# A two-layer graph attention kernel: 36 row gathers move into the prologue, and each of 36 steps computes one chunk of table rows itself

## The chip, the cores and the metric

The kernel runs on one core of one Trainium2 chip. The metric is the device time of one execution in microseconds (us). The core has a matrix engine (PE, with its weight loads PEld), a vector engine (DVE), a scalar engine (ACT), a general engine (POOL, GpSimd) that here mostly issues indirect DMAs, and SP, which issues plain DMAs. Each engine works through its own instructions in order and waits on semaphores of the others; 16 DMA engines carry all transfers.

## The reference, cut to what matters

The graph has N = 6250 nodes with 256 features and E = 200,000 edges sorted by destination, plus a self loop at every node. What is computed, in float32:

```
h  = relu(layernorm(x))                       # per node
for l, heads in ((0, 4), (1, 1)):
    hx  = x_l @ Wg                            # x_0 = h; 256 x 256, per node
    te  = relu(edge_attr @ We + be) * exp(x_l @ Wo + bo)[src]
    al  = leaky_relu((hx.as)[src] + (hx.ad)[dst] + (te @ Wge).ae, 0.2)
    al  = softmax of al over the edges of each dst
    out = segment_sum(hx[src] * al, dst) + b
    x_l+1 = relu(out + x_l) if l == 0 else out + x_l
return x + x_2 + h
```

## The kernel before

**Tables.** Every edge needs the row of its source node: hx (256 numbers), the logit parts and exp(x Wo + bo). The prologue (`prologue`) makes these rows once for all nodes and stores them in a DRAM table `T[0]`, 268 numbers a row; layer 0 makes the table `T[1]` for layer 1 as its nodes get done.

**Steps.** The edges are cut into 66 superchunks per layer: 64 of 24 chunks of 128 edges, and two short ones at the end (14 and 13 chunks), 1563 chunks in all. One superchunk of one layer is a step. `edges` writes the order of the work of all 132 steps out by hand; there is no scheduler. While step k (`st`) is computed, step k+1 (`nx`) is fetched and prepared, and the nodes of step k-1 (`pv`) are finished; `late` is the step whose T[1] rows are still to be multiplied and stored.

**The gather.** `gather(nx)` issues one indirect DMA on POOL per chunk: 128 table rows into `G[:, c, :]`. There are three G buffers, used in turn, so the gathers of step k+3 need the matmuls of step k to be done.

**Inside a step**, in order: `logits` (DVE, needs all chunks of G), `ends` (a PE transpose), `spread` and `parts` (one-hot masks and destination terms for `nx`), `rphase1` (edge features of `nx`: PE, ACT), `links` (two short scans on DVE and a PE transpose), `rows2(late)` (two PE matmuls for T[1]), `blocks`, `maxima` (DVE, ending with an Exp on ACT), `rphase2` and `adst` (PE), `scale` (layer 0: one 6.5 us DVE multiply; layer 1: 24 ACT copies), `carried`, `sums` (24 matmuls on PE), `rows3(late)` (bias add on DVE, stores on SP), `onehots(nx)`, `finish(pv)`, `evict`, `rows1(pv)` (PE transposes, ACT copy into `h1T`), `edge_rows(nx)`.

**The prologue.** 49 tiles of 128 nodes in 9 groups (2, 5, then 7 each, 5, 2 tiles). Per tile: layernorm statistics on DVE (`stats`), normalise on ACT (`norm`), two PE transposes and an ACT copy (`turn`), two PE matmuls (`mult`), bias add on DVE (`keep`). The reciprocal root of the variance is a bit trick and three Newton steps, on DVE for groups 0 to 2 and on POOL for groups 3 to 8. Per group, SP loads x (`load`) and stores the rows (`store`); three row buffers `trow` alternate. Then come 24 more tiles: the x rows that the 24 chunks of superchunk 0 need are gathered straight from x on POOL during the prologue (`first_rows`, `NX = 24`) into the first G buffer, and go through the same tile work in place. So step 0 needs no table; steps 1 to 131 do.

Of the kernel before, what the change touches and what calls it, by code (L numbers as in the profile page):

```python
# [31 lines left out]
P = 128  # L32
C = 24
SE = P * C
NX = 24
D = 256
ED = 32
PH = 64
# [41 lines left out]
class Kernel:  # L80
# [10 lines left out]
    def run(self):  # L91
        nc, tc = self.nc, self.tc
        self.cp = self.pool("consts")
        self.dp = self.pool("tables", space=DRAM)
        N = self.N
        self.T = [self.dp.tile([N + P, L.TW], F32, name=f"T{L.l}") for L in self.L]
        n, w = (self.NS + 1) // 2, self.L[1].TW + D
        self.nd = [self.dp.tile([n * (M + 1), w], F32, name=f"nd{i}") for i in range(2)]
        self.x1 = self.dp.tile([N + P, D], F32, name="x1")
        with ExitStack() as c:  # L100
            c.enter_context(tc.manual_schedule())
            self.gp = [self.pool("gath0", 1, c)]
# [3 lines left out]
            self.steps = [dict(L=L, s=s, C=self.cs[s], o=offs[s], k=L.l * self.NS + s)  # L106
                          for L in self.L for s in range(self.NS)]
            self.prologue()
            self.edges(c)
        self.general()  # L110


    def consts(self, wp):
# [5 lines left out]
        pool = (wp, cp)  # L119
        self.ones = cp.tile([P, 1], F32, name="ones")  # L120
        nc.gpsimd.memset(self.ones, 1.0)
        self.bias, self.webd, self.be, wge = [], [], [], []
        def weights(L):

# [79 lines left out]
    def prologue(self):  # L204
# [7 lines left out]
        with ExitStack() as c:  # L212
# [15 lines left out]
            src0 = wp.tile([P, CX], I32, name="src0", bufs=1)  # L228
            nc.sync.dma_start(src0, a["src"][:, 0:CX])
            for g in range(1, 3):  # L230
                load(g)
            first, later, more = self.consts(wp)
# [18 lines left out]
            self.G0 = G0 = self.gp[0].tile([P, C, 270], F32, name="G")  # L251

            def first_rows():
                for i in range(CX):
                    nc.gpsimd.indirect_dma_start(
                        out=G0[:, i, 0:D], out_offset=None, in_=a["x"][0:N, :],
                        in_offset=bass.IndirectOffsetOnAxis(ap=src0[:, i:i + 1], axis=0))
                    yield

            rows0 = first_rows()  # L260
# [5 lines left out]
            def stats(g):  # L266

                n, x = len(groups[g]), xs[g]
                w = GT if g < g0 else C
                st = wp.tile([P, w, 6], F32, name=f"st{w}", bufs=2 if g < g0 else 1)  # L270
                mv = wp.tile([P, w, 2], F32, name=f"mv{w}", bufs=3 if g < g0 else 1)
                s = wp.tile([P, 3, w], F32, name=f"sc{w}", bufs=3 if g < g0 else 1)
                for i in range(n):
                    V.bn_stats(st[:, i, :], x[:, i, :])
                    yield
                for i in range(n):
                    V.bn_aggr(mv[:, i, :], st[:, i, :])
# [6 lines left out]
                V.tensor_scalar(y.bitcast(I32), v.bitcast(I32), -0.5, float(0x5F3759DF), op0=OP.mult, op1=OP.add)  # L284
                yield
                V.tensor_scalar(v, v, -0.5, None, op0=OP.mult)
                yield
                e = nc.gpsimd if 3 <= g < g0 else V
                for _ in range(3):
                    e.tensor_mul(t, y, y)  # L290
# [5 lines left out]
                    if e is V:  # L296
                        V.scalar_tensor_tensor(y, t, 1.5, y, op0=OP.add, op1=OP.mult)
                        yield
                    else:
                        e.tensor_scalar(t, t, 1.5, None, op0=OP.add)  # L300
                        e.tensor_mul(y, t, y)
                e.tensor_copy(out[:, :, 0], y)
                if e is V:
                    V.scalar_tensor_tensor(out[:, :, 1], mv[:, :n, 0], -1.0, y, op0=OP.mult, op1=OP.mult)
                else:
                    e.tensor_mul(t, mv[:, :n, 0], y)
                    e.tensor_scalar(out[:, :, 1], t, -1.0, None, op0=OP.mult)
                yield

# [51 lines left out]
                        del ahead[q]  # L361

            index = self.indices(wp)
            kept = 0
# [279 lines left out]
    def edges(self, ctx):  # L644
# [30 lines left out]
        for k, st in enumerate(steps):  # L675
# [199 lines left out]
    def gather(self, st):  # L875
# [4 lines left out]
        for c in (range(0) if st["k"] == 0 and self.CX > last else (last, *range(last))):  # L880
            nc.gpsimd.indirect_dma_start(  # L881
                out=G[:, c, 0:L.TW], out_offset=None, in_=self.T[L.l][0:self.N, :],
                in_offset=bass.IndirectOffsetOnAxis(ap=idx[:, c:c + 1], axis=0))

    def pair(self, k):

# [411 lines left out]
        e.tensor_add(nrow, nrow, b)  # L1298
        yield

    def turned(self, st, wp, psum):
        pT = psum.tile([P, 512], F32, name="fin")
        for i in range(2):
            self.nc.tensor.transpose(pT[:, i * P:(i + 1) * P], st["x1"][:, i * P:(i + 1) * P], self.ident)
        st["hT"] = hT = wp.tile([P, 2, P], F32, name="h1T", bufs=1)
        self.nc.scalar.activation(hT.rearrange("p k n -> p (k n)"), pT[:, :2 * P], AF.Copy)  # L1306

# [168 lines left out]
def drain(g):  # L1476
    for _ in g:
        pass
# [22 lines left out]
def layout(inputs):  # L1501
# [23 lines left out]
    for s, c in enumerate(cs):  # L1525
        e0, e1 = o * P, (o + c) * P
        nx[e1 - 1] = END_DST
        for t, v in ((srcp, sp), (dstp, dp), (dnxp, nx)):
# [11 lines left out]
        o += c  # L1540
    a.update(gsrc=sp.reshape(-1, 1), gdst=gdst.reshape(-1, 1), gdrow=gdst,
             gea=np.ascontiguousarray(eap.T))
    a.update(src=srcp, dst=dstp, dnx=dnxp, drow=drow, prow=prow, sdst=sdst,
             dpv=np.ascontiguousarray(prow[:, 3].T),
             srow=np.ascontiguousarray(sp[:cs[0] * P].reshape(P, -1).T),
# [26 lines left out]
```

## Time and profile before

| | |
|---|---|
| median of 3 runs | 4050.89 us (4050.79 to 4054.03) |
| profiled execution | 4055.1 us, its span 4053.3 us |
| POOL busy | 2998.9 us (74%) |
| PE busy | 2639.2 us (65%) |
| DVE busy | 2436.3 us (60%) |
| ACT busy | 1117.1 us (28%) |
| granted PE clock, mean | 0.779 |

Busy time leaves out register, branch, semaphore and DMA-issuing instructions of SP; an indirect DMA on POOL does count. Times in the views count from the span's start. Layer 0 runs from about 115 to 2067 us and layer 1 from there to the end. A row of grouped instructions gives line, engine, operation, output and input, count, then busy us and mean ns of one, then the engine's idle time before them and what ended it. A timeline row gives start, length, engine, line, operation, output and input, count and, in brackets, the idle time before it with its releaser.

### The profile page before, as it was taken

What the parts mean: (1) busy time and instruction counts of PE and PEld (TensorE: products, weight loads), DVE (VectorE), ACT (ScalarE), POOL (GpSimd) and SP (SyncE); (2) the same over time, 40 slices, a digit from 0 to 9 for tenths busy, and PEclk for the clock granted to TensorE, in tenths of its full rate; (3) what the DMA queues carried; (4) which work ended last, traced back from release to release, by engine and by line L of the source; (5) the groups of instructions that cost most, each with busy time, mean ns of one, the idle gap of its engine ahead of it and who ended that gap; (6) DMA issues with size and microseconds to landing.
All of it is one profiled execution on the core that took longest, in us unless ns stands there. A gap on an engine that the chain in (4) does not pass through costs nothing.

```text
span 4053.3 us, 37237 instructions
## 1 busy us (share of the span) xinstructions
PE 2639.2 (65%) x9878; PEld 1719.8 (42%) x9878; DVE 2436.3 (60%) x6063; ACT 1117.1 (28%) x2670; POOL 2998.9 (74%) x3253
## 2 busy tenths in 40 slices
PE   8776766666666766766646656656656566566565
PEld 6454444444444444444433433434434334334343
DVE  7887877877877877877744434333344343343445
ACT  5211111111111111111123434434334344343341
POOL 5777777777777777777747777777777777777775
PEclk9888878888887888888777777777777777777777
DMA  7455555555555555555534455455445445445443
GB/s 246 135 158 143 150 155 144 150 154 146 149 154 149 147 152 151 146 151 153 138 108 134 136 143 142 131 142 141 134 139 141 135 138 144 132 138 143 134 136 96
DMA packets 239250, 583.15 MB, mean 144 GB/s; under 512 B 64235, under 2 KB 96401, under 8 KB 238971
## 3 DMA queue, kind: packets, MB, share of 16 engines
q0 software_dynamic: 150144, 422.75, 39.3%
q1 hardware_dynamic: 88477, 157.30, 12.1%
q8 instruction: 85, 1.39, 0.1%
q14 instruction: 128, 1.05, 0.1%
q10 hardware_dynamic: 416, 0.67, 0.1%
HBM read 542.72 MB, written 37.86 MB: 143 GB/s over the span
## 4 chain that ended last, share of the span: by engine, by line
POOL 33%; DVE 27%; issue 14%; ACT 9%; PE 9%; DMA 8%; DVEq 0%; SPq 0%; ACTq 0%; POOLq 0%
POOL G L881 33%; DVE G L1192 8%; DMA G<-T,src 7%; ACT G L1201 7%; PE y L981 4%; DVE S L1021 4%; PE u L1211 2%; DVE lb L1005 2%; PE ps L439 1%; DVE m L1140 1%; DVE rt L1070 1%; ACT R L982 1%; DVE al L1088 1%; DVE al L1086 1%; DVE fb L1101 1%
## 5 line engine op out<-in xcount | busy, mean ns | idle before, releaser
L881 POOL DMA_INDIRECT G<-T,src x3102 | 2946.7, 950 | 1003.3 <-issue 916.3
L1211 PE MATMUL u<-G,S 128*128 128x270 f32 (+1 forms) x6252 | 1569.1, 414 | 187.4 <-DVE G L1182 184.1
L1211 PEld LDWEIGHTS u<-G,S 128*128 128x128 f32 x6252 | 1279.1, 206 | 479.0 <-DVE G L1182 212.2
L1201 ACT ACTIVATE G<-G,kw 128x256 f32<-128x256 f32 x1512 | 609.0, 497 | 0.0
L982 ACT ACTIVATE R<-y,webd 128x1024 f32<-128x1024 f32 (+2 forms) x264 | 235.4, 892 | 1322.8 <-PE y L981 817.4
L1108 PE MATMUL lf<-ident,fb 128*36 128x128 f32 (+1 forms) x132 | 50.3, 381 | 821.3 <-DVE fb L1101 795.7
L1084 DVE TENSOR_TENSOR G<-rt,G 128x96 f32<-128x96 f32 (+1 forms) x132 | 30.3, 230 | 866.0 <-DMA G<-T,src 866.0
L1192 DVE TENSOR_TENSOR G<-G,kps 128x6144 f32<-128x6144 f32 (+3 forms) x77 | 440.9, 5734 | 0.0
L1021 DVE TENSOR_TENSOR S<-kps,loc 128x3072 f32<-128x3072 f32 x132 | 437.6, 3315 | 4.6
L981 PE MATMUL y<-ea,webd 64*128 64x256 f32 (+1 forms) x1056 | 393.7, 840 | 50.9 <-ACT R L982 50.9
L990 PE MATMUL zad<-R,wea 128*64 128x384 f32 (+1 forms) x1056 | 308.2, 726 | 158.5 <-ACT R L982 158.2
L1108 PEld LDWEIGHTS lf<-ident,fb 128*36 128x36 f32 (+1 forms) x132 | 15.8, 119 | 863.4 <-DVE fb L1101 837.0
L990 PEld LDWEIGHTS zad<-R,wea 128*64 128x64 f32 x1056 | 88.2, 189 | 428.3 <-ACT R L982 339.8
L1216 ACT ACTIVATE U<-u 128x270 f32<-128x270 f32 (+1 forms) x132 | 51.8, 393 | 631.0 <-PE u L1211 631.0
L1243 DVE SCALAR_TENSOR_TENSOR mg<-U,mw 128x1 f32<-128x1 f32 x66 | 14.5, 220 | 281.3 <-ACT mw L1241 281.3
L981 PEld LDWEIGHTS y<-ea,webd 64*128 64x128 f32 x1056 | 124.7, 289 | 123.7 <-ACT R L982 70.3
L1174 DVE SCALAR_TENSOR_TENSOR G<-U,kw,G 1x257 f32<-1x257 f32 x62 | 29.6, 478 | 185.1 <-ACT G L1201 185.1
L1070 DVE STREAM_TRANSPOSE rt<-zad 128x768 f32<-128x768 f32 (+1 forms) x130 | 126.1, 970 | 8.5 <-PE zad L1056 8.5
L1042 PE MATMUL zad<-a,Q 128*128 128x12 bf16 (+1 forms) x132 | 26.1, 197 | 156.6 <-DVE a L1037 156.2
L439 PE MATMUL fin<-wg,h1T 128*128 128x260 f32 x264 | 125.3, 623 | 3.7 <-ACT h1T L1306 3.7
L1005 DVE TENSOR_TENSOR lb<-lb,kps 128x1536 bf16<-128x1536 bf16 (+1 forms) x68 | 112.9, 1661 | 0.0
L1316 ACT ACTIVATE t1row<-t1row 128x1 f32<-128x1 f32 x66 | 13.4, 203 | 349.9 <-DVE t1row L443 349.9
(195 smaller groups left out, 2238.4 us busy)
## 6 DMA issues: line engine op xcount, KB each, us to landing
G<-T,src POOLq DMA_INDIRECT x3102, 2.8
ea<-in_ea_dram SPq DMA_DIRECT2D x64, 768.0 KB
lb<-locrow SPq DMA_DIRECT2D x64, 384.0 KB
nd<-t1row SPq DMA_DIRECT2D x66, 225.8 KB
tw<-nd SPq DMA_DIRECT2D x66, 225.8 KB
tw<-T SPq DMA_DIRECT2D x66, 117.2 KB
T<-t1row SPq DMA_DIRECT2D x66, 113.8 KB
tw<-in_x_dram SPq DMA_DIRECT2D x66, 112.0 KB
```

The lines of the kernel that those rows point to most:

```text
L439: self.nc.tensor.matmul(ps[:, :L.MW], hT[:, k, :], self.wg[L.l][:, k, :], start=(k == 0), stop=(k == 1))
L881: nc.gpsimd.indirect_dma_start(out=G[:, c, 0:L.TW], out_offset=None, in_=self.T[L.l][0:self.N, :], in_offset=bass.IndirectOffsetOnAxis(ap= ...
L981: nc.tensor.matmul(y[:, i, :n], self.webd[l][r, :], ea[r, w], start=True, stop=True)
L982: nc.scalar.activation(R[:, :, w], y[:, :, :n], AF.Relu, bias=self.be[l])
L990: nc.tensor.matmul(st["zad"][i * PH:(i + 1) * PH, o], self.wea[l][0], R[:, i, w], start=True, stop=False)
L1005: V.tensor_tensor(lb[:, :, :n], lb[:, :, :n], self.k_part.unsqueeze(2).to_broadcast([P, i, n]), op=OP.is_equal)
L1021: nc.vector.tensor_tensor(st["S"][:, c0:c1, :], self.k_iota.unsqueeze(1).to_broadcast(w), self.loc[:, o + c0:o + c1].unsqueeze(2).to_broad ...
L1070: V.transpose(rv[:, :32 * c].rearrange("p (b n) -> p b n", b=2), z.rearrange("p (b n) -> p b n", b=2)[:, :, :16 * c])
L1108: self.nc.tensor.transpose(self.lf[0:e.shape[1], 1:P + 1], e, self.ident)
L1192: nc.vector.tensor_tensor(v, v, pw[:, c0:c1, :].unsqueeze(3) .to_broadcast([P, c1 - c0, H, L.F]), op=OP.mult)
L1201: self.nc.scalar.activation(v, v, AF.Copy, scale=st["w"][:, c:c + 1])
L1211: nc.tensor.matmul(st["u"][:, :L.W], S[:, i, :], G[:, i, 0:L.W], start=(j == 0), stop=(j == c - 1))
```

## The change

- `NX` falls from 24 to 12: chunks 0 to 11 of superchunk 0 still come from x in the prologue; chunks 12 to 23 are gathered from the table after it. The prologue has 61 tiles instead of 73.
- For steps 1 to 36 of layer 0 (`early`), the prologue gathers the x rows of the last chunk on POOL, 36 gathers, into slots 12 to 23 of the first G buffer, used three times over; after every four gathers SP stores them to a DRAM tensor `xg` (9 stores of 512 KB). A slot is written again only when its store has landed. `begun < 7 + 17 * k // 20` paces the 48 prologue gathers over the tiles. A new input `srcx` holds their indices.
- In those 36 steps `gather` issues 23 indirect DMAs, and SP loads the 128 x rows from `xg` into `G[:, 23, :]` (128 KB, one plain DMA). The step then does the tile work for this chunk, for `nx`: `early_norm` behind `ends` (4 DVE and 13 ACT instructions), `early_turn` behind `blocks` (two PE transposes and an ACT copy into `h1T`), `early_mult` ahead of `rphase2` (two PE matmuls), `early_keep` ahead of `sums` (a DVE add, an ACT Exp).
- `rows2(late)` moves from behind `links` to ahead of `spread`, `rows3(late)` from behind `sums` to behind `links`, in all steps of both layers. The new work uses the same single `fin` buffer of PSUM and the same `h1T` as they and `rows1` do.
- In the prologue's Newton steps POOL keeps groups 3, 5 and 7; groups 4, 6 and 8 go to DVE, and the last Newton product is written in place of a copy.

```diff
-NX = 24
+NX = 12
+NB = 36
+EB = 4
...
             def first_rows():
-                for i in range(CX):
+                for i in range(NR):
+                    j = i - CX
+                    q = i if j < 0 else CX + j % NE
                     nc.gpsimd.indirect_dma_start(
-                        out=G0[:, i, 0:D], out_offset=None, in_=a["x"][0:N, :],
+                        out=G0[:, q, 0:D], out_offset=None, in_=a["x"][0:N, :],
                         in_offset=bass.IndirectOffsetOnAxis(ap=src0[:, i:i + 1], axis=0))
+                    b = j % EB
+                    if j >= 0 and (b == EB - 1 or i == NR - 1):
+                        nc.sync.dma_start(self.xg[:, j - b:j + 1, :], G0[:, q - b:q + 1, 0:D])
                     yield
...
-                e = nc.gpsimd if 3 <= g < g0 else V
+                e = nc.gpsimd if g in (3, 5, 7) and g < g0 else V
...
-                if 0 <= k < 10 or k >= 14 and k % 4 == 0:
+                while begun < 7 + 17 * k // 20:
+                    begun += 1
                     next(rows0, None)
...
             drain(self.logits(st))
             self.ends(st)
+            self.early_norm(nx)
+            if late:
+                self.rows2(late)
             self.spread(nx)
             self.parts(nx)
             y = self.rphase1(nx)
             next(y)
             self.links(st)
             if late:
-                self.rows2(late)
+                self.rows3(late)
+                late = None
             self.load_fl(k + 1)
             self.blocks(nx)
+            self.early_turn(nx)
             drain(self.maxima(st))
             drain(y)
+            self.early_mult(nx)
             self.load_ea(k + 2)
             self.rphase2(nx)
...
             self.carried(st)
+            self.early_keep(nx)
             self.sums(st)
-            if late:
-                self.rows3(late)
-                late = None
...
+        if L.l == 0 and st["s"] in self.early:
+            nc.sync.dma_start(G[:, last, 0:D], self.xg[:, self.early[st["s"]], :])
+            st["x"] = G[:, last, :]
+            order = range(last)
...
+    def early_norm(self, st):
+
+        if "x" not in st:
+            return
+        V, L, x = self.nc.vector, st["L"], st["x"][:, 0:D]
+        act = self.nc.scalar.activation
+        t = self.wp.tile([P, 12], F32, name="xt")
+        mean, var, y, q, b = (t[:, i:i + 1] for i in range(6, 11))
+        V.bn_stats(t[:, 0:6], x)
+        V.bn_aggr(t[:, 6:8], t[:, 0:6])
+        V.tensor_scalar(var, var, EPS, None, op0=OP.add)
+        V.tensor_scalar(y.bitcast(I32), var.bitcast(I32), -0.5, float(0x5F3759DF), op0=OP.mult, op1=OP.add)
+        act(var, var, AF.Copy, scale=-0.5)
+        act(mean, mean, AF.Copy, scale=-1.0)
+        for _ in range(3):
+            act(q, y, AF.Copy, scale=y)
+            act(q, q, AF.Relu, bias=self.c15, scale=var)
+            act(y, q, AF.Copy, scale=y)
+        act(b, mean, AF.Copy, scale=y)
+        st["h"] = h = self.np_.tile([P, D], F32, name="hw", bufs=2)
+        self.nc.scalar.activation(h, x, AF.Relu, bias=b, scale=y)
...
+    def early_mult(self, st):
+
+        if "x" in st:
+            st["t0"] = self.ps_f.tile([P, 512], F32, name="fin")
+            self.node_rows(st["L"], st["hT"], st["t0"])
+
+    def early_keep(self, st):
+
+        if "x" in st:
+            L, row = st["L"], st["x"]
+            self.node_store(L, st["t0"], row)
+            self.nc.scalar.activation(row[:, L.g:L.g + 1], row[:, L.g:L.g + 1], AF.Exp)
```

More of the change, by code (lines that the diff above doesn't have):

```diff
@@ L107, in run @@
                           for L in self.L for s in range(self.NS)]
+            n = min(NB, self.NS - 4) if self.cs[0] >= NX + EB else 0
+            self.early = {s: s - 1 for s in range(1, n + 1)}
+            if self.early:
+                self.xg = self.dp.tile([P, len(self.early), D], F32, name="xg")
             self.prologue()
@@ L121, in consts @@
         nc.gpsimd.memset(self.ones, 1.0)
+        self.c15 = cp.tile([P, 1], F32, name="c15")
+        nc.gpsimd.memset(self.c15, 1.5)
         self.bias, self.webd, self.be, wge = [], [], [], []
@@ L227, in prologue @@
             load(0)
-            src0 = wp.tile([P, CX], I32, name="src0", bufs=1)
-            nc.sync.dma_start(src0, a["src"][:, 0:CX])
+            NR, NE = CX + len(self.early), (self.cs[0] - CX) // EB * EB
+            src0 = wp.tile([P, NR], I32, name="src0", bufs=1)
+            nc.sync.dma_start(src0, a["srcx"][:, 0:NR])
             for g in range(1, 3):
@@ L287, in stats @@
                 yield
-                e = nc.gpsimd if 3 <= g < g0 else V
-                for _ in range(3):
+                e = nc.gpsimd if g in (3, 5, 7) and g < g0 else V
+                for i in range(3):
+                    z = out[:, :, 0] if i == 2 else y
                     e.tensor_mul(t, y, y)
@@ L295, in stats @@
                         yield
-                    if e is V:
-                        V.scalar_tensor_tensor(y, t, 1.5, y, op0=OP.add, op1=OP.mult)
+                        V.scalar_tensor_tensor(z, t, 1.5, y, op0=OP.add, op1=OP.mult)
                         yield
@@ L300, in stats @@
                         e.tensor_scalar(t, t, 1.5, None, op0=OP.add)
-                        e.tensor_mul(y, t, y)
-                e.tensor_copy(out[:, :, 0], y)
+                        e.tensor_mul(z, t, y)
                 if e is V:
-                    V.scalar_tensor_tensor(out[:, :, 1], mv[:, :n, 0], -1.0, y, op0=OP.mult, op1=OP.mult)
+                    V.scalar_tensor_tensor(out[:, :, 1], mv[:, :n, 0], -1.0, out[:, :, 0], op0=OP.mult, op1=OP.mult)
                 else:
-                    e.tensor_mul(t, mv[:, :n, 0], y)
+                    e.tensor_mul(t, mv[:, :n, 0], out[:, :, 0])
                     e.tensor_scalar(out[:, :, 1], t, -1.0, None, op0=OP.mult)
@@ L363, in prologue @@
             index = self.indices(wp)
-            kept = 0
+            kept, begun = 0, 6
             for k in range(-3, len(tiles) + 1):
@@ L879, in gather @@
         last = st["C"] - 1
-        for c in (range(0) if st["k"] == 0 and self.CX > last else (last, *range(last))):
+        first = self.CX if st["k"] == 0 else 0
+        order = (last, *range(first, last)) if first <= last else ()
+        if L.l == 0 and st["s"] in self.early:
+            nc.sync.dma_start(G[:, last, 0:D], self.xg[:, self.early[st["s"]], :])
+            st["x"] = G[:, last, :]
+            order = range(last)
+        for c in order:
             nc.gpsimd.indirect_dma_start(
@@ L883, in gather, with early_turn @@
                 in_offset=bass.IndirectOffsetOnAxis(ap=idx[:, c:c + 1], axis=0))
+    def early_norm(self, st):
[18 more added lines that the diff above has]
+        self.nc.scalar.activation(h, x, AF.Relu, bias=b, scale=y)
+    def early_turn(self, st):
+        if "x" in st:
+            self.turned(st, self.np_, self.ps_f, st["h"])
+    def early_mult(self, st):
[3 more added lines that the diff above has]
+    def early_keep(self, st):
+        if "x" in st:
+            L, row = st["L"], st["x"]
+            self.node_store(L, st["t0"], row)
+            self.nc.scalar.activation(row[:, L.g:L.g + 1], row[:, L.g:L.g + 1], AF.Exp)
     def pair(self, k):
@@ L1299, in nodes0, with turned @@
         yield
-    def turned(self, st, wp, psum):
+    def turned(self, st, wp, psum, x=None):
+        x = st["x1"] if x is None else x
         pT = psum.tile([P, 512], F32, name="fin")
         for i in range(2):
-            self.nc.tensor.transpose(pT[:, i * P:(i + 1) * P], st["x1"][:, i * P:(i + 1) * P], self.ident)
+            self.nc.tensor.transpose(pT[:, i * P:(i + 1) * P], x[:, i * P:(i + 1) * P], self.ident)
         st["hT"] = hT = wp.tile([P, 2, P], F32, name="h1T", bufs=1)
@@ L1542, in layout @@
              gea=np.ascontiguousarray(eap.T))
+    early = [offs + c - 1 for offs, c in zip(np.cumsum([0] + cs).tolist(), cs)][1:NS - 3]
+    a.update(srcx=np.ascontiguousarray(srcp[:, [*range(min(cs[0], NX)), *early[:NB]]]))
     a.update(src=srcp, dst=dstp, dnx=dnxp, drow=drow, prow=prow, sdst=sdst,
```

## The prediction

> **What bounds the kernel now.** I read the page first (busy shares by engine, the 40 slices, the group of gathers), then who waited for whom on POOL, then POOL's instructions in order of time. The page:
>
> ```profile
> PE 2639.2 (65%) x9878; PEld 1719.8 (42%) x9878; DVE 2436.3 (60%) x6063; ACT 1117.1 (28%) x2670; POOL 2998.9 (74%) x3253
> POOL 5777777777777777777747777777777777777775
> L881 POOL DMA_INDIRECT G<-T,src x3102 | 2946.7, 950 | 1003.3 <-issue 916.3
> ```
>
> POOL looks only 74% busy, evenly. But of the 1003.3 us in which it stood idle before a gather, 916.3 are "issue": it waited for nothing. The waits of POOL say the same, and give the three real stops:
>
> ```profile
> POOL G L881 <- issue: 916.3, 3008, 0.3
> POOL G L881 <- DMA T<-t1row: 40.1, 1, 40.1
> POOL G L881 <- DMA tw<-in_x_dram: 14.3, 1, 14.3
> POOL G L881 <- ACT pen L972: 4.8, 1, 4.8
> ```
>
> 40.1 us is the change of layer, where the table must be complete. The other two lie at the start. In order of time on POOL:
>
> ```profile
> 72.73 0.95 POOL L255 DMA_INDIRECT G<-in_x_dram,src  x1 [0.30 <-issue]
> 88.01 0.94 POOL L881 DMA_INDIRECT G<-T,src  x1 [14.34 <-DMA tw<-in_x_dram]
> 89.26 0.95 POOL L881 DMA_INDIRECT G<-T,src  x1 [0.31 <-issue]
> ...
> 147.01 0.94 POOL L881 DMA_INDIRECT G<-T,src  x1 [0.30 <-issue]
> 152.73 0.95 POOL L881 DMA_INDIRECT G<-T,src  x1 [4.78 <-ACT pen L972]
> ```
>
> A gather costs 1.25 us from start to start (88.01 to 89.26). POOL starts when the stores of T[0] have landed, runs 48 gathers (steps 1 and 2) to 147.01, and stops once, at step 3, for the first G buffer, which step 0 still uses. So the end is: start of the table gathers, plus 1.25 us for each of 3102, plus the stops, plus a tail. Everybody else waits for POOL. DVE's wait in the whole run, then in layer 0 from 400 to 1200 us, then busy times there (PE, PEld, DVE, ACT, POOL):
>
> ```profile
> DVE G L1084 <- DMA G<-T,src: 866.0, 121, 19.6
> ```
> ```profile
> DVE G L1084 <- DMA G<-T,src: 131.5, 26, 9.6
> ```
> ```profile
> 800.00:1200.00 400.00, 270.74 (x989) 176.41 (x986) 310.98 (x671) 55.02 (x131) 303.11 (x319) 0.82 0.54 151
> ```
>
> In layer 0 a step lasts 24 x 1.25 = 30.0 us, so 800 us are 26.7 steps, and DVE waits 131.5 / 26.7 = 4.9 us a step for gathers. Its own work with its small waits takes 25.1 us. That is the room the change has in a step.
>
> **The change part by part.**
>
> *Gathers after the prologue.* 36 steps issue 23 instead of 24: 36 x 1.25 = -45.0 us. Step 0 gathers 12 chunks from the table that came from x before: 12 x 1.25 = +15.0 us. Net -30.0 us of POOL, if POOL stays the bound.
>
> *The stop at step 3* (4.8 us) goes. Step 0 needed its G buffer until 152; with POOL 15 us of gathers later at step 3 and step 0 having 12 tiles less to wait for, the buffer is free well before: -4.8 us. What is late next there is POOL itself.
>
> *The start of the table gathers.* The prologue gets 48 instead of 24 x gathers, nine stores to xg, and two chains between them. Rows of the prologue: two of POOL in order of time around a Newton block, the landing of x gathers, the last three stores of T on SP, the first 88 us and a full stretch (PE to POOL busy, then PE clock, DMA share, GB/s), and the two DMA queues in the first 88 us:
>
> ```profile
> 29.27 0.21 POOL L290 TENSOR_TENSOR sc<-sc 128x7 f32<-128x7 f32 x1 [3.34 <-DVE sc L284]
> 33.68 1.07 POOL L255 DMA_INDIRECT G<-in_x_dram,src  x1 [0.17 <-issue]
> ```
> ```profile
> DMA to landing us min/median/max: 2.7/5.5/8.5
> ```
> ```profile
> 74.81 8.39 SPq L344 DMA_DIRECT2D T<-trow  x3
> ```
> ```profile
> 0.00:88.00 88.00, 75.62 (x344) 55.88 (x344) 72.55 (x325) 50.43 (x129) 50.23 (x149) 0.98 0.78 257
> 30.00:40.00 10.00, 8.80 (x46) 6.84 (x45) 5.01 (x22) 6.52 (x18) 3.70 (x14) 1.00 1.04 266
> ```
> ```profile
> q1 hardware_dynamic: 6063, 18.67, 62.5%
> q0 software_dynamic: 1152, 3.15, 12.3%
> ```
>
> A Newton block takes POOL 33.68 - 29.27 = 4.4 us. The new order on POOL is 13 gathers, block 3, 12 gathers, block 5, 11 gathers, block 7, 12 gathers. From the end of block 3 at 33.7: 33.7 + 15.0 + 4.4 + 13.8 + 4.4 + 15.0 = 86.3, if nothing holds it. The last gather starts at 85.0 and lands 5.5 later, at 90.5; then its store is issued, and only behind it, SP being in order, the last store of T. That one was issued at 83.2 before (74.81 + 8.39) and the table gathers started 4.8 us after it. So by this chain the start is about 90.9 + 4.8 = 95.7, 7.7 us later. What queues behind the waiting SP: every store of T from group 2 on (some 6 us later each, with three row buffers in between), and the loads of ea and lb, which step 0 needs only after 100 us. What queues behind POOL's gathers: block 7, done at 71 instead of 64.7, which may hold PE for a few us; the late store of T hides that. Groups 4, 6 and 8 add 10 short instructions each to DVE, which hide in the same way.
>
> The other limit is the DMA engines. They are busy 0.78 x 88 = 68.6 us. 24 more x gathers at 0.123 x 88 / 24 = 0.45 us add 10.8; 4.72 MB of stores at 0.625 x 88 / 18.67 = 2.95 us per MB add 13.9. That is 93.3 us of transfers before the table is whole: at a share of 1.0, as from 30 to 40 us, a start at 94; at the old share of 0.78, a start at 119.6. These two and the chain bound it: 88 (all hidden) to 119.6. I take 99, nearest to the chain with queueing at the end, where three stores of T, the ea load and the last gathers now meet: +11 us.
>
> The Trainium skill ("DMA: Bandwidth & Descriptors", section on the anatomy of one DMA) gives 2.0 us plus bytes / 436 GB/s for a GpSimd DMA, an estimate of 2.3 us for these 131 KB. By that the chain would start 3 us earlier and the sum be some 3 us lower; the trace has 5.5 us as the median here and 2.7 at least, and decides.
>
> *A step's own new work.* Groups that price it (the prologue's statistics on G, a small scalar and the bias add on DVE; a small, a wide and a copying ACT instruction), the spread mask, and one step in order of time:
>
> ```profile
> L274 DVE BATCH_NORM_STATS2 st<-G 128x6 f32<-128x256 f32 x24 | 9.0, 412 | 0.0
> L277 DVE BATCH_NORM_AGGREGATE mv<-st 128x2 f32<-128x6 f32 x73 | 6.5, 151 | 0.0
> L286 DVE TENSOR_SCALAR sc<-sc 128x7 f32<-128x7 f32 (+4 forms) x11 | 1.9, 171 | 0.2
> L443 DVE TENSOR_TENSOR t1row<-fin,bias 128x260 f32<-128x260 f32 x27 | 11.0, 409 | 0.0
> L1316 ACT ACTIVATE t1row<-t1row 128x1 f32<-128x1 f32 x66 | 13.4, 203 | 349.9 <-DVE t1row L443 349.9
> L1272 ACT ACTIVATE hw<-tw 128x256 f32<-128x256 f32 x66 | 38.6, 585 | 0.0
> L1306 ACT ACTIVATE h1T<-fin 128x256 f32<-128x256 f32 x66 | 25.0, 378 | 7.6 <-PE zad L1042 6.8 <-PE fin L1304 0.8
> ```
> ```profile
> 971.65 1.73 DVE L1005 TENSOR_TENSOR lb<-lb,kps 128x1536 bf16<-128x1536 bf16 x1
> ```
> ```profile
> 1004.74 0.33 DVE L1101 TENSOR_TENSOR_SCAN fb<-pen,al 128x96 f32<-128x96 bf16 x1
> 1005.13 0.40 PE L1108 MATMUL lf<-ident,fb 128*36 128x128 f32 x1 [6.00 <-DVE fb L1101]
> 1005.32 0.22 PE L1042 MATMUL zad<-a,Q 128*128 128x12 bf16 x1
> 1005.47 1.23 PE L981 MATMUL y<-ea,webd 64*128 64x256 f32 x4
> 1006.52 0.32 PE L1125 MATMUL lf<-ident,cl 36*128 36x36 f32 x1
> 1006.77 2.10 PE L439 MATMUL fin<-wg,h1T 128*128 128x260 f32 x4
> ```
>
> DVE gets 0.41 + 0.15 + 2 x 0.17 + 0.41 = 1.3 us. On PE the 2.10 us of `rows2` now stand ahead of the links' transpose (1006.52), for which `maxima` on DVE waits: it moves to about 1005.13 + 0.40 + 2.10 + 0.22 + 1.23 = 1009.1, 2.5 us later, which contains the norm's 0.9 but not the keep's 0.41: 2.9 us in such a step. In the steps with the spread mask (every second) DVE's 1.73 us cover most of it, and 1.3 remain. Mean 2.1: DVE needs 27.2 us a step, against 23 x 1.25 = 28.75 of POOL. The cost is nothing, hidden by the gather with 1.5 us to spare. If nothing of ACT were hidden, 12 x 0.203 + 0.585 + 0.378 = 3.4 us come on top: 30.6 us, 1.85 over. Nearest is 27.2, because ACT is busy only 55 us of 400 and its chain starts before the masks and links that the Exp waits for anyway.
> PE's two transposes and two matmuls lie in the 6.5 us in which DVE scales; PE is at 68% and no bound. The xg load is issued on SP behind the row loads of the step; DVE would wait in `early_norm` if it came late. `rows3` moved earlier costs nothing in layer 1 either: DVE waits for gathers there too (866.0 in all).
>
> **Sum.** -45.0 + 15.0 - 4.8 + 11 = -23.8 us. The profiled execution took 4055.1 us, so 4031.3 against itself. It is 4.2 us above the median of the runs shown, 4050.9; the forecast for the median is **4027.1 us**.
>
> **The rivals** (times against that median).
> - *The prologue's additions hide wholly.* Start at 88: -34.8, 4016.1. For it: POOL idles 14.3 us before 88. Against: the chain of landings on SP above.
> - *The prologue stays at its old DMA share.* Start at 106 to 119.6: -16.8 to -3.2, 4034 to 4047.7. For it: SP now stops nine times for landings, and waits of slots, stores and blocks can chain up. Against: the transfers are independent of PE, whose pace left the share at 0.78.
> - *Slower: DVE becomes the bound in the 36 steps.* Place: `maxima` behind ACT's 13 instructions and PE's new order. At 30.6 us a step DVE falls behind by 36 x 1.85 = 67 us. POOL can run ahead by about a step, 30 us, before G buffers stop it (the rows above show 48 gathers ahead of step 0), and steps 37 on give it back. So 37 us are lost: +13, 4064. It decides from 28.75 + (30 + 23.8) / 36 = 30.2 us a step.
> - *The saved gathers are worth nothing* because POOL's time goes elsewhere: about 4051 plus the start, up to 4062. Against: POOL waits for nothing for 3000 gathers.
>
> **Chances.** The forecast (start 92 to 106, so 4020 to 4034) 0.62; all hidden 0.13; the long prologue 0.12, half of it within 0.2% (8.1 us, about what a measurement here can tell from no change); DVE the bound 0.09; worth nothing 0.04, mostly within. Faster 0.62 + 0.13 + 0.06 = 0.81; same 0.09; slower 0.10. The range that leaves out two in ten, with the hidden case at its edge and most of the long prologue: 4015 to 4044; the forecast's own is 4020 to 4034.
>
> **What would show it.** Table gathers start at 95 to 103, not 88; no stop at step 3; in steps 1 to 36 POOL's only waits are "issue", and DVE's wait for gathers shrinks from 4.9 to about 1.5 us a step; the stop at the change of layer stays near 40. Wrong if POOL stops in the steps for sums or ACT, if that last stop grows, or if the start lies beyond 106.

## The result and the profile after

The changed kernel takes 4085.95 us (median of 4 runs, 4085.11 to 4087.61), the kernel before 4052.46 us beside it: ratio 1.0083, 95% interval 1.0065 to 1.01. It is slower by 0.8%; forecast was 4027.1 us. The profiled execution of the changed kernel has a span of 4085.8 us, that of before 4053.3.

The page, then the waits of POOL in the whole run (us in total, times, longest):

```profile
PE 2679.9 (66%) x10022; PEld 1732.2 (42%) x10022; DVE 2468.6 (60%) x6232; ACT 1256.6 (31%) x3186; POOL 2992.5 (73%) x3206
...
L905 POOL DMA_INDIRECT G<-T,src x3078 | 2928.6, 951 | 1035.9 <-issue 902.6
```
```profile
POOL G L905 <- issue: 902.6, 2962, 0.6
POOL G L905 <- ACT h1T L1371: 47.0, 17, 6.1
POOL G L905 <- DMA T<-t1row: 40.2, 1, 40.2
POOL G L905 <- DMA T<-trow: 15.7, 1, 15.7
```

24 gathers fewer are there, as promised (3078, and 24 more of x), but POOL has a new kind of stop: 17 times, 47.0 us, for a G buffer that the step three before still uses. The row names a copy on ACT as the releaser, but these stops end 0.77 us after the last matmul of `sums`, as the one stop at step 3 does in the kernel before; the copy happens to end near by. So POOL isn't the bound everywhere any more. Who is, the waits of DVE from 400 to 1200 us say, and its busy time there (the answer of before was one line: 131.5 us for gathers):

```profile
DVE xt L917 <- DMA G<-xg: 87.8, 17, 10.6
DVE G L1225 <- ACT kps L1221: 33.4, 18, 2.5
DVE mg L1319 <- ACT mw L1317: 7.1, 26, 0.3
```
```profile
800.00:1200.00 400.00, 283.55 (x1057) 181.80 (x1056) 318.57 (x734) 110.09 (x325) 285.70 (x301) 0.82 0.54 149
```

DVE no longer waits for a gather at all. In the 800 us lie 26 loads from xg, so 26 steps of 30.8 us; in the mean DVE waits 87.8 / 26 = 3.4 us a step for the new rows (in 17 of the 26 steps) and 33.4 / 26 = 1.3 us for the Exp. The remaining 26.1 us are its own work and small waits, which were 25.1 before. One step shows where both waits come from: SP, DVE and ACT in order of time.

```profile
784.75 0.27 SPq L1415 DMA_DIRECT2D nd<-t1row  x1
800.41 0.33 SPq L1014 DMA_DIRECT2D tw<-in_x_dram  x1
800.94 0.33 SPq L1015 DMA_DIRECT2D tw<-T  x1
801.37 0.61 SPq L970 DMA_DIRECT2D lb<-locrow  x1
802.35 0.35 SPq L901 DMA_DIRECT2D G<-xg  x1
```
```profile
800.42 0.42 DVE L1362 TENSOR_TENSOR t1row<-t1row,fb 128x256 f32<-128x256 f32 x1
...
805.10 0.33 DVE L1165 TENSOR_TENSOR_SCAN fb<-pen,al 128x96 f32<-128x96 bf16 x1
810.40 0.43 DVE L917 BATCH_NORM_STATS2 xt<-G 128x6 f32<-128x256 f32 x1 [4.97 <-DMA G<-xg]
...
817.13 0.32 DVE L1225 COPY G<-kps 128x96 f32<-128x96 f32 x1 [2.48 <-ACT kps L1221]
```
```profile
811.46 0.20 ACT L921 ACTIVATE xt<-xt 128x1 f32<-128x1 f32 x1 [4.28 <-DVE xt L920]
811.57 0.19 ACT L922 ACTIVATE xt<-xt 128x1 f32<-128x1 f32 x1
811.66 0.28 ACT L924 ACTIVATE xt<-xt 128x1 f32<-128x1 f32 x1
811.97 0.39 ACT L925 ACTIVATE xt<-xt,c 128x1 f32<-128x1 f32 x1
...
815.19 0.60 ACT L929 ACTIVATE hw<-G,xt 128x256 f32<-128x256 f32 x1
...
816.85 0.25 ACT L1221 ACTIVATE kps<-mt 128x100 f32<-128x100 f32 x1
```

SP stands until 800.41, when finish on DVE frees the row buffer for the next row loads; these, then 384 KB of lb, and only then the xg load, issued at 802.35. DVE is at `early_norm` 3 us later and waits until 810.40, 8 us after the issue. ACT's twelve small instructions take 3.7 us (811.46 to 815.19). From the fourth on each needs the one before it, and they start 0.31 to 0.42 us apart, where the first three start 0.1 apart. Those with a scale or a bias read from a column are also longer, 0.28 to 0.39 us, where I had taken 0.203 from a single one without. Behind them come the wide normalisation and four more operations, the copy of the turned rows last, and only then the Exp.

The start: POOL, then SP in order of time (the second number of a row of several covers them all).

```profile
54.08 0.94 POOL L266 DMA_INDIRECT G<-in_x_dram,src  x1 [5.70 <-DVE trow L457]
...
91.30 0.95 POOL L266 DMA_INDIRECT G<-in_x_dram,src  x1 [0.30 <-issue]
107.98 0.94 POOL L905 DMA_INDIRECT G<-T,src  x1 [15.73 <-DMA T<-trow]
```
```profile
94.77 0.39 SPq L271 DMA_DIRECT2D xg<-G  x1
95.26 1.84 SPq L357 DMA_DIRECT2D T<-trow  x2
98.15 0.38 SPq L271 DMA_DIRECT2D xg<-G  x1
98.62 1.29 SPq L357 DMA_DIRECT2D T<-trow  x1
```

The table gathers start 20.0 us later, not 11. Counting the gathers off in order of time, the last one of step 3 stands 26.6 us behind that of the kernel before, the last one of step 20 only 10.9, the last one of step 37 again 27.3, the last one of layer 0 33.2, and so to the end. So POOL first runs ahead, as the saved gathers let it, and then the G buffers stop it: against the pace of the kernel before, the 1.25 us that each of the steps saves POOL are all lost again by step 37, and after it some 6 us more go.

### The profile page after: what moved, and what is told of

Read it like the earlier page. It is cut to its first block, busy times and chain, and to the rows that moved or that the text cites. A ratio compares the mean times of both kernels' runs of the same rounds, so it can differ in the third digit from the quotient of the medians.

```text
span 4085.8 us, 38508 instructions
## 1 busy us (share of the span) xinstructions
PE 2679.9 (66%) x10022; PEld 1732.2 (42%) x10022; DVE 2468.6 (60%) x6232; ACT 1256.6 (31%) x3186; POOL 2992.5 (73%) x3206
## 4 chain that ended last, share of the span: by engine, by line
POOL 30%; DVE 24%; issue 13%; ACT 13%; PE 11%; DMA 9%; DVEq 0%; SPq 0%; ACTq 0%; POOLq 0%
POOL G L905 29%; ACT G L1265 9%; DVE G L1256 7%; PE u L1275 6%; DMA G<-T,src 5%; PE y L1045 4%; DMA G<-xg 3%; DVE lb L1069 2%; DVE S L1085 2%; DVE rt L1134 1%; ACT R L1046 1%; PE ps L453 1%; DVE m L1204 1%; ACT xt L925 0%; DVE fb L1389 0%
## 5 line engine op out<-in xcount | busy, mean ns | idle before, releaser
L1275 PE MATMUL u<-G,S 128*128 128x270 f32 (+1 forms) x6252 | 1550.6, 410 | 177.1 <-DVE G L1246 173.0
L1275 PEld LDWEIGHTS u<-G,S 128*128 128x128 f32 x6252 | 1265.7, 204 | 463.9 <-DVE G L1246 203.0
L1054 PE MATMUL zad<-R,wea 128*64 128x384 f32 (+1 forms) x1056 | 324.8, 760 | 116.3 <-ACT R L1046 115.9
L453 PE MATMUL fin<-wg,h1T 128*128 128x260 f32 (+1 forms) x408 | 158.6, 526 | 10.1 <-ACT h1T L1371 9.7
L1317 ACT ACTIVATE mw<-mw 128x8 f32<-128x8 f32 x66 | 13.8, 209 | 467.7 <-DVE mw L1316 467.7
L453 PEld LDWEIGHTS fin<-wg,h1T 128*128 128x128 f32 x408 | 94.2, 255 | 83.3 <-issue 33.0
```

Of the source, the lines that this page charges most:

```text
L453: self.nc.tensor.matmul(ps[:, :L.MW], hT[:, k, :], self.wg[L.l][:, k, :], start=(k == 0), stop=(k == 1))
L1054: nc.tensor.matmul(st["zad"][i * PH:(i + 1) * PH, o], self.wea[l][0], R[:, i, w], start=True, stop=False)
L1275: nc.tensor.matmul(st["u"][:, :L.W], S[:, i, :], G[:, i, 0:L.W], start=(j == 0), stop=(j == c - 1))
```

## The experiments

Each kernel ran on one chip with the kernel before beside it; the ratio is against those runs. The diffs are cut to the lines that matter, and `...` marks what is left out. On two of the chips the kernel before itself takes 4835 and 4849 us, with PE as the bound: the waits of PE there have, for `best` (below), this line, where the kernel before on the other chips has none of its kind.

```profile
PE u L1303 <- issue: 1256.6, 665, 3.6
```

There gathers set no pace, and five kernels that met such a chip ran again on another; only the second runs are told below. (The first: the two rows calls 1.0044, three operations ahead of finish 1.0128, the mended steps 1.0366 and 1.037.) The version that ends up fastest is slower on such a chip: 1.0219 without and 1.0238 with its last edit.

**The load from xg a step ahead.** The theory: DVE became the bound because the load lands late and ACT's chain stands ahead of the Exp. The rivals: rows2 ahead of the links, or the prologue alone.

```diff
...
+            self.xg_load(steps[k + 2])
             self.load_ea(k + 2)
...
```

> The changed kernel, but a step's load from xg is issued one step earlier on SP (just ahead of the ea load of the step before, where its G buffer is already free), so it no longer stands behind the tw and lb loads. Theory (DVE became the bound because the xg load lands late, 3.4 us a step): the wait of DVE for it goes from 110 us to nearly nothing in the whole run, a step of 1 to 36 takes about 28.75 us (POOL's 23 gathers) instead of 30.8, and what stays is the late start of the table gathers: 4052.5 - 45.0 + 15.0 - 4.8 + 20 = about 4038 us. Rival (ACT's thirteen instructions ahead of the Exp, or rows2 ahead of the links on PE, hold DVE): the wait moves to the Exp or to the links, a step stays above 30 us, and the time above 4065 us.

4054.18 us, ratio 0.9985 (0.9976 to 0.9995), some 40 us less than the changed kernel by ratio. The waits of DVE from 400 to 1200 us:

```profile
DVE G L1161 <- DMA G<-T,src: 47.0, 20, 7.5
DVE G L1238 <- ACT kps L1234: 26.7, 16, 2.5
```

The wait for xg is gone and DVE waits for gathers again, though the Exp still comes late: POOL sets the pace. The step's theory holds, but of the forecast gain 9 us are missing (below: the gathers got longer).

**The norm behind `maxima`.** The load stays late; the chain is moved.

```diff
-            self.early_norm(nx)
...
-            self.early_turn(nx)
             drain(self.maxima(st))
             drain(y)
-            self.early_mult(nx)
+            self.early_norm(nx)
...
             self.adst(nx)
+            self.early_turn(nx)
+            self.early_mult(nx)
...
-            self.early_keep(nx)
             self.sums(st)
             self.onehots(nx)
+            self.early_keep(nx)
```

> The changed kernel, but early_norm is issued behind maxima and the last eviction of rphase1, the turn and the multiplication behind adst, and the keep behind the next step's onehots; the load from xg stays where it is. Theory (late xg load, and ACT's chain ahead of the Exp): DVE reaches the new rows some 6 us later, when they have mostly landed, and the Exp stands ahead of the chain; both waits (3.4 and 1.3 us a step) go, a step takes 28.75 us, the time is about 4038 us. Rival (rows2 ahead of the links on PE is what slows DVE): a step stays near 30 us, about 4070 us. If the load is later than I read, part of the wait stays and the time lies between, 4045 to 4060 us.

4052.82 us, 0.9983 (0.9974 to 0.9993). The same window:

```profile
DVE G L1148 <- DMA G<-T,src: 45.3, 22, 7.6
DVE xt L917 <- DMA G<-xg: 9.2, 6, 2.6
```

DVE reaches the rows later, when most have landed, and the wait for the Exp falls from 33.4 to 0.5 us. The gain is again some 8 us short of the forecast. Either edit takes DVE back under POOL's pace. The two waits together took 4.7 us a step, where 2.65 (28.75 less 26.1) had room, so it needed both.

**The prologue alone, and no early rows at all.**

```diff
-        if L.l == 0 and st["s"] in self.early:
+        if L.l == 0 and st["s"] in ():
```

> The changed kernel, but no step uses xg: all 24 chunks of each step are gathered from the table. The prologue with its 48 x gathers, its stores to xg, its 12 chunks for step 0, and the new places of rows2 and rows3 stay. Theory: table gathers start at 108 instead of 88 us (+20), step 0 gathers 12 more (+15.0), the stop at step 3 goes (-4.8): 4052.5 + 30 = about 4083 us, which would say that all of the 36 x 1.25 = 45 us that the changed kernel saves on POOL are lost again in its steps. Rival (the prologue costs little and the steps cost more than before): 4060 us or less.

4111.1 us, 1.0129 (1.0113 to 1.0146). This kernel stands 36.8 us behind the kernel before at the end of step 37, where the changed one stood 27.3: beside it the 36 early chunks still gain something.

```diff
-NB = 36
+NB = 0
```

> The changed kernel with NB = 0: 12 x gathers in the prologue for step 0, none for other steps, no xg, no stores of it, 24 table gathers in every step; the new places of rows2 and rows3 and the divided Newton blocks stay. Theory (the 36 gathers and stores make the late start): start at 84 to 88 us, 12 more table gathers (+15.0), no stop at step 3 (-4.8): 4059 to 4063 us. Rival (the order of rows2 and rows3, or the new Newton blocks, cost by themselves): 4070 us or more.

4086.39 us beside 4059.58, 1.0067 (1.005 to 1.0084). Both are slower than my terms allow, by 21 and by 16 to 20 us. The terms of the start are right: with NB = 0 the first table gather starts at 88.6 us, step 1 ends 15.9 us later than before, step 3 11.0 (+0.6, +15.2, -4.8). But then the distance grows through layer 0, from 11.0 at step 3 to 26.3 at its end, while nobody waits for anything new: the gathers themselves take longer. What these kernels still share with the changed one, behind the prologue, is the place of rows2 and rows3.

**That place alone,** in the kernel before.

```diff
             self.ends(st)
+            if late:
+                self.rows2(late)
...
             self.links(st)
             if late:
-                self.rows2(late)
+                self.rows3(late)
+                late = None
...
             self.sums(st)
-            if late:
-                self.rows3(late)
-                late = None
```

> The kernel before with rows2 ahead of spread and links and rows3 behind links, once more: the first time the chip ran the kernel before itself at 4835 us, with PE as the bound, where gathers set no rhythm. On a chip that runs it near 4050 us: theory (position of finish in the 1.25 us rhythm of the gathers) mean pitch in layer 0 up from 1.2575 to about 1.265 us, ratio 1.002 to 1.0035; rival (the move costs nothing) 1.000.

4068.51 us beside 4051.94, 1.0037 (1.0023 to 1.0051): a part that I had put at nothing costs 15 us. The group of gathers from 1300 to 2000 us (busy us, mean ns of one), before, with the two calls moved, and, from the next run, with three operations added ahead of finish:

```profile
L881 POOL DMA_INDIRECT G<-T,src x557 | 530.8, 953 | 169.7 <-issue 163.3 <-DVE mg L1259 2.4 <-DVE mw L1261 0.6
```
```profile
L881 POOL DMA_INDIRECT G<-T,src x555 | 532.8, 960 | 169.1 <-issue 163.0 <-DVE mw L1261 2.4 <-DVE cnt L1227 0.9
```
```profile
L909 POOL DMA_INDIRECT G<-T,src x557 | 531.8, 955 | 169.7 <-issue 165.1 <-DVE mg L1325 2.1 <-DVE shift L744 0.9
```

In order of time, POOL and DVE with the two calls moved: which gathers are long.

```profile
1515.43 0.95 POOL L881 DMA_INDIRECT G<-T,src  x1 [0.30 <-issue]
1516.68 1.16 POOL L881 DMA_INDIRECT G<-T,src  x1 [0.30 <-issue]
1518.14 1.06 POOL L881 DMA_INDIRECT G<-T,src  x1 [0.30 <-issue]
```
```profile
1516.60 0.42 DVE L1286 TENSOR_TENSOR fa<-fa,hw 128x256 f32<-128x256 f32 x1
1517.05 0.43 DVE L1288 TENSOR_TENSOR fb<-fa,fb 128x256 f32<-128x256 f32 x1
1517.39 0.42 DVE L1296 TENSOR_TENSOR t1row<-tw,hw 128x256 f32<-128x256 f32 x1
1517.96 0.42 DVE L1298 TENSOR_TENSOR t1row<-t1row,fb 128x256 f32<-128x256 f32 x1
```

The kernel lays its tiles in two memories of the core, SBUF and PSUM. The long gathers are mostly those that run beside finish's six wide operations, whose two inputs both lie in SBUF: from 200 to 2000 us, with the two calls moved, 105 of the 142 such gathers take over 1.0 us, of the 1280 others 37. In the kernel before it is 47 of 174 and 29 of 1257.

DVE is released in each step by a gather, so finish falls at a nearly fixed place in POOL's 1.25 us rhythm, and the order of the work before it decides which. Of the operation `fb<-fa,fb`, 34 of 61 start within 0.2 us of a gather's start in the kernel before, and 32 of 59 at 0.8 to 1.0 us, where the gather is about to end, with the calls moved. Over layer 0 (200 to 2000 us) the distances between gathers exceed 1.2515 us by 8.2 us in all before, 20.9 here and 23.0 with NB = 0. With the load ahead and with the norm behind `maxima` it is 17.4 and 17.8, some 9 more than before, about what the gains of those two runs fell short of their forecasts (9 and 8).

The Trainium skill ("SBUF — State Buffer", section on who interferes with whom) has the rule: a DVE instruction with two SBUF inputs contends with a GpSimd instruction that reads SBUF. The trace agrees, with 0.95 us becoming 1.06 to 1.16. So does the multiply of `scale`, 6.5 us long, whose second input `kps` lies not in SBUF but in PSUM: in the kernel before, 266 gathers lie wholly inside it, and none takes over 0.96 us. No run changed the inputs of finish alone, so the rule isn't tested by itself.

**The place in the rhythm.** The kernel with NB = 0, and more work for DVE.

```diff
...
+            if pv and st["L"].l == 0:
+                for _ in range(3):
+                    nc.vector.tensor_scalar(self.shift, self.ones, 1.0, None, op0=OP.add)
             if pv:
                 drain(self.finish(pv))
```

> The kernel with NB = 0 and three small DVE operations ahead of finish in layer 0, once more on a chip that runs the kernel before near 4050 us. Theory (position of finish in the rhythm): excess of layer 0's gathers over the common pitch falls from 23 us to 8 to 14, ratio 1.003 to 1.0045 beside 1.0067 without the three operations. Rival (the place of rows3, or its stores, makes gathers long): ratio 1.006 to 1.008.

4073.68 us, 1.0053 (1.0036 to 1.007), between the theory's range and the rival's. 39 of 59 of the `fb<-fa,fb` now start within 0.2 us of a gather's start, and the excess falls from 23.0 to 11.9 us. In the times the step is half as large, 26.8 to 21.7 us over the kernel before, and the two intervals overlap: the trace shows the mechanism, the times only agree with it.

**A mending that failed.** rows2 and rows3 back at their places; then the new rows' turn, which shares their PSUM buffer, comes behind the sums.

```diff
...
             self.onehots(nx)
+            self.early_turn(nx)
+            self.early_mult(nx)
             if pv:
                 drain(self.finish(pv))
```

> The mended step (rows2 and rows3 at their old places, the load from xg one step ahead, early_norm behind maxima, turn and multiplication behind the sums, keep behind finish), once more on a chip that runs the kernel before near 4050 us. Theory: POOL sets the pace in steps 1 to 36, -45.0 + 15.0 - 4.8 + 20 = -14.8 us, ratio 0.9965, or 0.999 if finish falls badly in the rhythm. Rival (PE's multiplication behind the sums holds the next links): ratio 1.003 or more, as the 1.037 on the slow chip suggests.

4256.78 us, 1.0503 (1.0486 to 1.0521). From 400 to 1200 us DVE's great wait is

```profile
DVE mg L1332 <- ACT mw L1330: 214.8, 23, 9.9
```

The copy of the turned rows stands on ACT ahead of finish's Exp and waits for PE's sums. I had named PE's multiplication as the rival, and it was ACT's queue.

**Stores to xg one group later on SP,** on top of that kernel.

```diff
-                        nc.sync.dma_start(self.xg[:, j - b:j + 1, :], G0[:, q - b:q + 1, 0:D])
+                        full.append((j - b, j + 1, q - b, q + 1))
+                        if len(full) > 1:
+                            xg_store()
```

> The mended step with each store to xg one group of four gathers later on SP and the last one behind the last store of T, once more on a chip that runs the kernel before near 4050 us. Theory (SP's order made the start late): table gathers start at 95 to 101 us instead of 108, ratio 7 to 13 us below the mended step alone. Rival (DMA load or the row engines are the limit): start at 105 or later, as the 120.6 beside 118.6 on the slow chip suggests.

4250.54 us, 1.0489 (1.0471 to 1.0506). Only the start is read: 105.0 us beside 109.2. SP's order is worth 4 us here, less than the 7 I asked for. On the chip of the first runs, with PE as the bound, the same edit went 2 us the other way, from 118.6 to 120.6.

**No stores at all,** all steps from the table.

> As the run with the prologue alone (48 x gathers, all steps gather 24 chunks from the table), and the nine stores to xg are left out, so the 36 gathered chunks are thrown away. Theory (the stores make the late start: on SP they wait for landings ahead of the table's stores, and they are 4.7 MB on the DMA engines): table gathers start at 92 to 97 us instead of 106.5, time 10 to 14 us below that run, ratio near 1.010. Rival (the x gathers themselves, on POOL and the DMA engines, make it): start at 103 or later, ratio 1.012 to 1.013.

4089.26 us, 1.0089 (1.0073 to 1.0104). The first table gather, with the prologue alone and then without its stores:

```profile
106.48 0.94 POOL L905 DMA_INDIRECT G<-T,src  x1 [15.91 <-DMA T<-trow]
```
```profile
93.53 0.94 POOL L903 DMA_INDIRECT G<-T,src  x1 [6.92 <-DMA tw<-in_x_dram]
```

So of the 18.5 us the stores make 13.0, and the rest of the prologue's change, 24 more gathers of x above all, 5.5. Part of the 13.0 is on POOL itself: without stores the last x gather starts at 85.66 and no x gather stops; with the prologue alone it starts at 89.62, because the 25th, the first that writes a slot again, stands 4.7 us. Its row names an operation on DVE, but as the stop is gone without the stores, it is the store of that slot it waits for.

**Both step edits, and the last three stores behind the last store of T.**

```diff
-                        if len(full) > 1:
+                        if len(full) > 1 and i < NR - 2 * EB:
```

> The changed kernel with both mendings of the step (load from xg one step ahead; early_norm behind maxima, turn and multiplication behind adst, keep behind the onehots), and in the prologue each store to xg one group of four gathers later and the last three behind the last store of T. Theory: each alone gave 4053 to 4054 us where the kernel before had 4059.6; together they cannot give more than POOL's pace, so the same -6, and the start at 99 to 103 instead of 108 gives -5 to -9 more: ratio 0.996 to 0.9975. Rival (DMA load makes the start): start 105 or later, ratio 0.998 to 0.9985.

4043.77 us, 0.9978 (0.9969 to 0.9987); start at 104.9, beside the rival's 105 and not within the theory's 99 to 103.

**And rows2 and rows3 at their old places** wherever the next step has no chunk from xg.

```diff
-            if late:
+            if late and "x" in nx:
                 self.rows2(late)
...
```

> As both_late_store, and rows2 and rows3 are at their old places in every step whose successor has no chunk from xg (steps 36 on, and all of layer 1). Theory (the early place of rows2 and rows3 lengthens the gathers by about 0.16 us a step): -3 to -5 us more over steps 37 to 65, ratio 0.995 to 0.9965, 4035 to 4042 us beside a kernel before of 4055. Rival: ratio as both_late_store.

4037.66 us, 0.9962 (0.9948 to 0.9976). The mean gather from 1300 to 2000 us is 954 ns, beside 960 in the run before it. The start, SP and POOL:

```profile
93.71 4.49 SPq L266 DMA_DIRECT2D xg<-G  x3
99.05 0.37 SPq L1042 DMA_DIRECT2D tw<-in_x_dram  x1
99.84 0.34 SPq L1043 DMA_DIRECT2D tw<-T  x1
```
```profile
104.46 0.94 POOL L933 DMA_INDIRECT G<-T,src  x1 [11.92 <-DMA tw<-T]
```

The table is complete at 99.84, where SP's own load from it goes, yet POOL starts 4.6 us later. What the row names as the releaser, a load of rows for finish, is nothing that a gather needs; but step 0's first gather goes into the slot that the last store to xg reads. The next run tests that.

**That slot last.**

```diff
-        order = (last, *range(first, last)) if first <= last else ()
+        order = () if first > last else range(first, last + 1) if first else (last, *range(last))
```

> best_slots once more, on a chip that runs the kernel before near 4052 us. Theory (step 0's slots held the start of best at 104.5 us): start at 99.5 to 101.5 us, ratio 0.9948 to 0.9958, 4031 to 4036 us. Rival (the DMA engines hold it): start at 104 or later, ratio 0.996 to 0.9965. On a chip where PE is the bound the ratio says nothing on either, and only the start is read.

4032.86 us beside 4053.4, ratio 0.9952 (0.9938 to 0.9965). On one of the two chips with PE as the bound it moved the start from 118.3 to 115.3; here, POOL:

```profile
89.17 0.95 POOL L272 DMA_INDIRECT G<-in_x_dram,src  x1 [0.30 <-issue]
99.33 0.94 POOL L933 DMA_INDIRECT G<-T,src  x1 [9.22 <-DMA tw<-in_x_dram]
```

The start is the 99 of the forecast, and the profiled span, 4029.1 us, lies 24.2 below that of before. On a chip that runs the kernel before near 4050 us this version beats both kernels.

## Why the prediction was wrong, point by point

- *Gathers -45.0 and +15.0; the stop at step 3, -4.8.* Step 0's gathers and the stop came as written (the NB = 0 kernel, +15.2 and -4.8). The 36 gathers are saved only while POOL is the bound, which was the condition; it failed.
- *A step's own new work at 27.2 us, hidden.* This is the step that failed. DVE's own work grew to 26.1, less than forecast; the term left at zero was the two waits, 4.7 us a step, and with them POOL's time: its 17 stops, 47.0 us, less the 0.3 us that stand ahead of any gather, are 41.9 of the 45.0 us. "DVE would wait in `early_norm` if it came late" was written down without a time for the load, though the order on SP (behind the rows that finish frees, and behind lb) was readable: 8 us from issue to landing against 3 us on DVE. ACT's chain was priced at 0.203 us an instruction, as if none waited for another, and was to start "before the masks and links that the Exp waits for anyway"; it ends behind them and pushes the Exp, and did so even with the load on time (26.7 us from 400 to 1200 us). 30.8 us a step resulted.
- *The slower rival* had most of the mechanism (DVE the bound, ahead of the Exp, POOL's lead used up first, decisive from 30.2 us a step) at a chance of 0.09 and 4064 us. That its 30.6 us a step lie so near 30.8 is luck: they count ACT's work as hidden nowhere, and the late load, 3.4 of the 4.7 us, isn't in it. With 30.8 its own working gives 36 x 2.05 - 30 = 43.8 us lost. Counted by positions, 42 us of the 45 were lost (33.2 - 20.0 - 15.2 + 4.8 + 45.0 - 5.9 = 41.9). Of the 58.9 us between forecast and result these are the largest part; 9.0 more are the start, 5.9 the longer gathers behind step 37, and the kernel before took 1.6 more beside it.
- *The saved gathers are worth nothing,* at a chance of 0.04, came near in effect, but its 4051 to 4062 us leave out the +15.0 and the -4.8 of the same forecast; with them and the +11 it would have been 4072.
- *The start +11.* The place was right (SP's landings, DMA load), the size not: +20.0, as in the rival of the long prologue. In the chain, the last x gather was to start at 85.0 "if nothing holds it" and started at 91.30, since the 25th stood 5.7 us (54.08) for the store of its slot; its store went out 6.9 us behind it, not 5.5; and POOL started 8.1 us after the last store of T was issued (98.62 + 1.29), not 4.8. The stores make 13 of the 18.5 us with the prologue alone. Some 2 to 4 come from their order ahead of T's, and some 5 in `best` from G slots they still read; neither that wait nor the 25th gather's was in the forecast. How the rest divides between the DMA engines and SP was not tried.
- *rows2 and rows3 cost nothing.* Wrong. No engine waits for them, but they move finish in POOL's rhythm: 15 us in the kernel before, about 6 in the changed kernel, where only steps 38 to 65 are at POOL's pace.
- *The stop at the change of layer stays near 40:* 40.2. *Layer 1 unaffected:* so it is.

Of the signs named, the start beyond 106 and stops of POOL in the steps both came. With the three causes mended the forecast's sum comes out within 6 us (4032.9 against 4027.1, ratio 0.9952 against 0.9941). That the start is again 99 is luck: the forecast had it with all stores to xg ahead of the last store of T, and here three come behind it.

## What to carry to other kernels

A load that a step newly waits for needs a time of its own: when its queue reaches it, what stands ahead of it, and when it lands, against the moment its reader arrives. Small instructions that each need the one before cost more than as many without dependence, and what stands ahead of an engine's next urgent instruction is on the path. And where an engine that issues gathers is the bound, the work of another engine beside it isn't free: the place of that work in the rhythm can be worth as much as the edit.

## What was not expected of the hardware

- A gather on POOL of 0.95 us takes up to 1.16 us in the rows above beside 128x256 f32 operations of two SBUF inputs on DVE; moving these by half a microsecond changed layer 0 by some 11 us of excess.
- On ACT, 128x1 instructions that each need the one before start 0.31 to 0.42 us apart, beside 0.1 for the three that need none; with a scale, or a scale and a bias, read from a column they take 0.28 and 0.39 us, beside 0.20 without.
- On two chips PE stood idle, in the runs there, 1107 to 1259 us in 593 to 669 stops before matmuls of the sums without waiting for anything the profile shows; the same edits turned from -0.4% to +2.2% there. Why is open.
